# Attention and gated feed-forward in one kernel: K/Q and O/V weight loads issued at different places of the unit loop

## The chip, the cores and the metric

The kernel runs on one core of one Trainium2 chip. The metric is the device time of one execution in microseconds (us); lower is better. Engines are named as in the profile: PE (matmuls), PEld (its weight loads), DVE, ACT, POOL, and SP, which here computes nothing and issues every DMA.

## The reference, cut to what matters

Shapes: x is 16 x 256 x 256 (4096 tokens of width 256), 16 heads of 128, feed-forward width 2048 with 4-bit weights that are expanded first.

```python
def attn(x):
    q = einsum('bpd,hde->bphe', x, W_Q) + b_Q          # k and v likewise
    scores = einsum('bqhe,bkhe->bhqk', q, k) / sqrt(128)
    attn = softmax(where(causal, scores, -1e5), axis=-1)
    z = einsum('bkhe,bhqk->bqhe', v, attn)
    return einsum('bqhe,hed->bqd', z, W_O) + b_O

x = x + layernorm(attn(layernorm(x)))
x = x + layernorm(ffn(layernorm(x)))      # ffn: gelu(x Wg) * (x Wu), then Wd
```

## The kernel before, in words

Every fp32 matrix is kept as a rounded part and a remainder, and every product is three matmuls (`mm3`, line 353). The weights are split into the two parts once, in the first block of tokens (`w_split`, line 298), and written to DRAM (`w_keep`, line 324, some slots later, through the list `late`). In every later block they are read back, already split, by `w_get` (line 332): 512 KB for each of K, Q, O and for each half of a V tile. Each weight has two tiles in turn (`w_tile`, line 290).

The attention is cut into 128 **units**: 8 blocks of 512 tokens, 8 pairs of heads in each, 2 heads in a pair (`units`, `pairs`). The main loop runs `for i in range(-4, N + 2)` and works on several units at once; `p = i // 2` is the pair, and i is even for the first head of a pair. In the order of the program, one pass i does:

- `st_s(i+3)`: scores and the exponentials of unit i+3; then `st_qk(i+4)`: K and Q products of unit i+4 (weights K and Q of pair (i+4)//2).
- `st_t(i+3)`: DVE transposes the probabilities into `tr`.
- `st_o(p-1, i%2)`: output product of pair p-1 (weight O); `st_z(i)`: probabilities times V for unit i, which needs `ph` (ACT) and `pl` (POOL).
- `st_p(i+1)`: `ph` and `pl` of unit i+1, from `pt`; `st_v(i+4)`: V products, a quarter of those of two pairs (weight V).
- `st_b(i+2)`: SP issues the read `pt<-hop` (384 KB) of unit i+2; it must wait until the four writes of that unit have landed.
- `st_w(i+3)`: SP issues the four writes `hop<-tr` (96 KB each) of unit i+3.

So the probabilities of a unit go out to DRAM at the end of one pass and come back at the end of the next, and ACT, POOL and PE use them one and two passes after that. Between the stages stand calls of `slot`, in which side jobs advance by a step: layer norms of other blocks (which issue `xhop`, `xr`, `ohop`, `o`, `xs` and `x1d` transfers), the weight splits of the first block, the expansion of the feed-forward weights (`f_make`, `f_scale`, with the loads `ld` and the writes `fg`, `fu`, `fd`).

In the profile every computing instruction stands under line 99 (`run`) and every DMA issue under line 91 (`dma`), so the tile names tell them apart. `dma` ties each DMA to the one before it, so SP issues all of them in the order of the program. `w_get` of a later block also calls `overdue(now[0] + 4)`, which issues pending writes up to four slots early.

Where the weights are fetched (`weights`, defined after the first tokens are ready): at the end of odd passes, after `st_w`, O of pair p+1 and a V half for pair p+5; at the start of the next even pass, K and Q of pair p+3. Between the two stands only one `slot`, so the four loads are neighbours: 2 MB every second pass, none in the other. After the attention, the same core runs the feed-forward (the loop over `NGRP`).

Of the kernel before, what the change touches and what calls it, by code (L numbers as in the profile page):

```python
# [28 lines left out]
def kernel(  # L29
# [30 lines left out]
    def f(ap):  # L60
        return ap.bitcast(F32)
# [24 lines left out]
    def dma(dst, src):  # L86
        if queue[0] is None:
            queue[0] = nc.sync.dma_start(dst, src).ins
            return
        with tc.issue_after(queue[0]):  # L90
            queue[0] = nc.sync.dma_start(dst, src).ins  # L91
# [33 lines left out]
    def add(jobs, job, kind):  # L125
        jobs.append([job, 0, kind])

    def overdue(time):
        while late and late[0][0] <= time:
            _, do, args = late.popleft()  # L130
            do(*args)

    def slot(kinds, *lanes):

        now[0] += 1
        overdue(now[0])
        for jobs in lanes or (splits, urgent, behind, made, spare, idle):
            if step(jobs, kinds):
                return
# [91 lines left out]
    def ln1(b):  # L231
        xs = [x_load(x, b, hf) for hf in range(2)]
        yield V_, 7
        mv, rs = yield from ln_stats([xs[hf][:, t, :] for hf in range(2) for t in range(2)])
        xn = wide("xn")
        for t in range(4):
            yield G_
            ln_apply(xn[:, t, :], xs[t // 2][:, t % 2, :], mv, rs, t)
        yield V_
        hop = dram.tile([P, 4, 2 * P], F32, tag="xhop", name="xhop", bufs=2)  # L240
        yield from turn_tokens(hop, xn)
        yield N_, 5
        yield from split_tokens((1, b), hop)
# [46 lines left out]
    def w_tile(n):  # L290
        return wp.tile([P, 2, 1024 if n == "v" else 512], F32R, tag=f"w{n}", name=f"w{n}", bufs=2)

    def w_view(w):
        return w.rearrange("p s (k c) -> p s k c", k=2)
# [3 lines left out]
    def w_split(p, n):  # L298

        raw = RAW.pop((p, n)).rearrange("p (k c) -> p k c", k=2)  # L300
        key, done = p, True
        if n == "v":
            key, done = p // 2, p % 2
            w = HALF.pop(key) if done else w_tile(n)
            if not done:
                HALF[key] = w
            wv_ = w_view(w)[:, :, :, (p % 2) * 256 : (p % 2 + 1) * 256]
        else:
            w = w_tile(n)
            wv_ = w_view(w)  # L310
        c = qscale if n == "q" else 1.0
        run(nc.scalar.activation, wv_[:, 0], raw, AF.Copy, scale=c)
        if n in "vo":
            run(nc.gpsimd.tensor_tensor, wv_[:, 1], raw, f(wv_[:, 0]), ALU.subtract)
        else:
            run(nc.vector.scalar_tensor_tensor, wv_[:, 1], raw, c, f(wv_[:, 0]), ALU.mult, ALU.subtract)
        ahead = p + (2 if n == "v" else 1)
        if ahead < NG:
            w_raw(ahead, n)
        if done:  # L320
            W[key, n] = w_view(w)
            late.append((now[0] + 4, w_keep, (key, n, w)))
# [5 lines left out]
    def split(p, n):  # L328
        w_split(p, n)
        yield from ()  # L330

    def w_get(p, n):

        if p < NG:
            add(splits, split(p, n), A_ if n in "vo" else V_)
        elif p < len(pairs):
            overdue(now[0] + 4)
            if n == "v":
                key, part = p // 2, p % 2
                w = HALF.pop(key) if part else w_tile(n)  # L340
                HALF[key] = w
                dma(f(w[:, part]), WD[key % (NG // 2), n][:, part])
                if part:
                    W[key, n] = w_view(HALF.pop(key))
            else:
                w = w_tile(n)
                dma(f(w), WD[p % NG, n])
                W[p, n] = w_view(w)
# [110 lines left out]
    def st_t(u):  # L459


        pr = PR.pop(u)
        tr = work.tile([P, 4, 6, 32], F32, tag="tr", name="tr")
        run(
                nc.vector.transpose,
                tr.rearrange("p k m i -> p m k i"), pr.rearrange("p c b (k j) -> p (c b) k j", k=4)
            )
        TR[u] = tr
# [11 lines left out]
    def st_p(u):  # L480
        pt = PT.pop(u).rearrange("p a m i -> p m a i")
        ph = work.tile([P, 2, 2, P], F32R, tag="ph", name="ph")
        pl = work.tile([P, 2, 2, P], F32R, tag="pl", name="pl")
        four = [t.rearrange("p c b (a i) -> p (c b) a i", a=4) for t in (ph, pl)]
        run(nc.scalar.copy, four[0], pt[:, 0:4])
        run(nc.gpsimd.tensor_tensor, four[1], pt[:, 0:4], f(four[0]), ALU.subtract)
        PH[u] = (ph, pl, pt)
# [102 lines left out]
    def f_load(g, n):  # L590
        psrc, ssrc = FSRC[n]
        ld = work.tile([P, 2, 256], F32, tag="raw", name="ld", bufs=6)
        pk, sc = ld[:, 0, :].bitcast(I32), ld[:, 1, :]
        dma(pk, psrc[g])
        dma(sc, ssrc[g].unsqueeze(1).to_broadcast([8, 16, 256]))
        LD[g, n] = pk, sc

    def f_make(g, n, then):


        pk, sc = LD.pop((g, n))

        def small_tile(dtype, name):
            return work.tile([P, 2, 256], dtype, tag="code", name=name, bufs=4)

        c = work.tile([P, 2, 256], I32, tag="raw", name="codes", bufs=6)
        sg, t, v = small_tile(BF16, "sg"), small_tile(BF16, "t"), small_tile(BF16, "v")
        run(nc.vector.tensor_scalar, c[:, 0, :], pk, 15, None, ALU.bitwise_and)
        run(nc.vector.tensor_scalar, c[:, 1, :], pk, 4, 15, ALU.arith_shift_right, ALU.bitwise_and)
        yield V_  # L610
        if then:
            f_load(*then)
        run(nc.vector.tensor_scalar, sg, c, 8.0, -2.0, ALU.is_ge, ALU.mult)
        yield V_
        run(nc.vector.tensor_scalar, c, c, 7, None, ALU.bitwise_and)
        yield V_
        run(nc.vector.tensor_scalar, t, c, 2.0, 8.0, ALU.mult, ALU.subtract)
        yield V_
        run(nc.vector.scalar_tensor_tensor, v, c, 0.5, t, ALU.mult, ALU.max)
        yield V_  # L620
        run(nc.vector.scalar_tensor_tensor, v, c, 2.0, v, ALU.subtract, ALU.max)
        yield V_
        run(nc.vector.scalar_tensor_tensor, v, sg, 1.0, v, ALU.add, ALU.mult)
        add(made, f_scale(g, n, v, sc), G_)
# [316 lines left out]
    run(nc.gpsimd.tensor_scalar, bqs, bqk[:, 0, :], qscale, 1.0, ALU.mult, ALU.mult)  # L941
    for p in range(2):
        w_split(p, "v")
    w_get(2, "v")

    def weights(*of):
        for pn, n in of:
            if pn > {"o": -1, "v": 2}.get(n, 0):
                w_get(pn, n)

    for i in range(-4, N + 2):
        p = i // 2
        odd = i % 2 == 1
        if p >= 0 and not odd and p < len(pairs):
            b, g = pairs[p]
            if g == 0 and b + 1 < NBLK:
                add(urgent, ln1(b + 1), N_)
            if b == 0 and g == 7:
                pieces = [(fg, n) for fg in range(NG) for n in "gud"]
                f_load(*pieces[0])  # L960
                for m, piece in enumerate(pieces):
                    add(idle, f_make(*piece, pieces[m + 1] if m + 1 < len(pieces) else None), V_)
            if b == NBLK - 1 and g == 0:
                add(spare, x_ops(0), N_)
        if not odd:
            weights((p + 3, "k"), (p + 3, "q"))
        if 0 <= i + 3 < N:
            st_s(i + 3)
        slot(V_)
        if i + 4 < N:  # L970
            st_qk(i + 4)
        slot(V_, urgent, behind)
        slot(G_)
        slot(G_)
        if 0 <= i + 3 < N:
            st_t(i + 3)
        if 0 <= p - 1 < len(pairs):
            st_o(p - 1, i % 2)
        if 0 <= i < N:
            st_z(i)  # L980
        if 0 <= i + 1 < N:
            st_p(i + 1)
        if i + 4 < N:
            st_v(i + 4)
        elif after:
            run(*after.popleft())
        if 0 <= i + 2 < N:
            st_b(i + 2)
        if 0 <= i + 3 < N:
            st_w(i + 3)  # L990
        if odd:
            weights((p + 1, "o"), (p + 5, "v"))
        slot(A_ + G_)
        if N - 9 <= i < N - 7:
            f_get(0, "ug"[i - (N - 9)])
        if i >= N - 3:
            for name in (("m1",), ("m2",), ("m6",), (), ())[i - (N - 3)]:
                part(0, name)
# [93 lines left out]
```

## Time and profile before

| | |
|---|---|
| median of 3 runs | 1564.98 us (1562.86 to 1571.53) |
| profiled execution, its own time | 1558.9 us |
| its span, first to last instruction | 1556.9 us |
| mean granted PE clock | 0.994 |
| DMA moved | 407.54 MB, mean 262 GB/s |
| attention units, first K matmul of the first to that of the last | 10.9 to 1025.8 us |

How to read it: busy shares are averages over the whole span; in the views by stretch, a row gives the length, then each engine's busy time and number of instructions, the granted clock, the busy share of the 16 DMA engines and the rate. In a timeline a row gives start, duration, engine, operation, out<-in, and in brackets the idle time of the engine before it with what ended it. "SPq" is SP's queue of issues; its duration is that of the issue, not of the transfer.

### The profile page before, as it was taken

The numbers are of one execution on the slowest core, as the hardware profiler recorded it, in microseconds if no ns is written. First come the engines' busy times: TensorE is split into PE (matmuls) and PEld (weight loads), VectorE is DVE, ScalarE is ACT, GpSimd is POOL, SyncE is SP. The second block draws the span as 40 slices with busy tenths as digits, with TensorE's granted clock in tenths as the row PEclk, the third lists the DMA queues.
The fourth block names the chain that finished last, engine by engine and source line by source line (L and its number), as shares of the span: only waits on it lengthen the run. The fifth ranks groups of instructions, "written<-read, shape, count | busy, mean of one in ns | idle before, by whom it ended". The sixth has DMA issues, their size and how long they took to land.

```text
span 1556.9 us, 25639 instructions
## 1 busy us (share of the span) xinstructions
PE 1514.1 (97%) x7792; PEld 1278.6 (82%) x7792; DVE 1180.7 (76%) x2944; ACT 1028.6 (66%) x2600; POOL 807.1 (52%) x1017
## 2 busy tenths in 40 slices
PE   8999999999999999999999999999999999999996
PEld 6888888888888887888888888877788878878885
DVE  5775888877788786877877777867877777787765
ACT  5876666766767675766675666766566665665663
POOL 3754668667667765856875875981420230240100
PEclk9999999999999999999999999999999999999998
DMA  7998799998998988889889898986557555645551
GB/s 270 317 311 274 248 312 304 296 289 285 291 297 287 321 270 293 279 285 314 276 262 318 263 319 271 308 293 253 189 204 252 194 230 198 242 189 215 220 194 41
DMA packets 200409, 407.54 MB, mean 262 GB/s; under 512 B 21456, under 2 KB 128464, under 8 KB 189520
## 3 DMA queue, kind: packets, MB, share of 16 engines
q1 hardware_dynamic: 200272, 405.91, 76.7%
q8 instruction: 62, 1.02, 0.3%
q14 instruction: 75, 0.61, 0.1%
HBM read 294.15 MB, written 111.67 MB: 261 GB/s over the span
## 4 chain that ended last, share of the span: by engine, by line
PE 72%; DMA 11%; DVE 6%; ACT 5%; SPq 3%; issue 2%; POOL 1%; DVEq 0%; POOLq 0%; ACTq 0%
PE pd L99 11%; PE pk L99 9%; PE pv L99 8%; PE pq L99 8%; PE po L99 8%; PE sc L99 7%; PE pz L99 7%; PE pa L99 7%; PE pf L99 5%; DMA pt<-hop 4%; SPq L91 3%; DVE sum L99 3%; PE pe L99 2%; DMA hop<-tr 2%; DMA wq<-wq 1%
## 5 line engine op out<-in xcount | busy, mean ns | idle before, releaser
L99 POOL TENSOR_TENSOR pl<-pt,ph 128x512 fp32r<-128x512 f32 x128 | 165.0, 1289 | 246.2 <-ACT ph L99 234.9
L99 POOL TENSOR_SCALAR pr<-pr,rc 128x128 f32<-128x128 f32 (+1 forms) x512 | 248.6, 501 | 65.5 <-DVE rc L99 65.4
L99 ACT ACTIVATE pr<-sc,mn 128x128 f32<-128x128 f32 (+1 forms) x512 | 208.9, 422 | 74.4 <-DVE mn L99 68.2
L99 DVE CUSTOM_DVE_ANT_0 sc<-sc,mask 128x128 f32<-128x128 f32 (+1 forms) x512 | 180.5, 373 | 48.7 <-PE sc L99 39.6
L99 PE MATMUL pv<-wv,xT 128*128 128x512 f32 x768 | 210.2, 409 | 0.0
L99 PE MATMUL pd<-inter,wd 128*128 128x512 f32 x768 | 200.4, 394 | 5.3 <-ACT inter L99 4.0
L99 PE MATMUL pk<-xT,wk 128*128 128x512 f32 x768 | 200.4, 396 | 2.7 <-DMA wk<-wk 1.7
L99 PE MATMUL pq<-xT,wq 128*128 128x512 f32 x768 | 197.3, 392 | 0.1
L99 POOL TENSOR_TENSOR rs<-rs,mhalf 128x4 f32<-128x4 f32 (+1 forms) x33 | 35.1, 1063 | 288.9 <-DVE rs L99 288.9
L99 PEld LDWEIGHTS pd<-inter,wd 128*128 128x128 f32 x768 | 143.0, 189 | 42.8 <-DVE inter L99 7.0
L99 PEld LDWEIGHTS pq<-xT,wq 128*128 128x128 f32 x768 | 144.9, 189 | 33.5 <-PE pk L99 0.5
L99 ACT ACTIVATE zh<-pz,bqk 128x512 fp32r<-128x512 f32 x128 | 89.2, 697 | 116.3 <-PE pz L99 116.2
L99 PE MATMUL po<-zh,wo 128*128 128x512 f32 x512 | 157.7, 389 | 0.0
L99 PEld LDWEIGHTS pk<-xT,wk 128*128 128x128 f32 x768 | 135.8, 189 | 26.3 <-DMA wk<-wk 1.9
L99 PEld LDWEIGHTS pv<-wv,xT 128*128 128x128 f32 x768 | 135.8, 190 | 23.8
L99 ACT CAST ph<-pt 128x512 fp32r<-128x512 f32 x128 | 79.4, 620 | 113.0 <-DMA pt<-hop 112.1
L99 ACT COPY part<-pa 128x512 f32<-128x512 f32 x192 | 112.0, 586 | 62.4 <-PE pa L99 59.8
L99 ACT CAST inter<-sum 128x512 fp32r<-128x512 f32 x128 | 80.1, 626 | 101.1 <-DVE sum L99 101.0
L99 DVE TENSOR_TENSOR inter<-sum,inter 128x512 fp32r<-128x512 f32 x128 | 92.2, 720 | 58.9 <-ACT inter L99 55.9
L99 DVE SCALAR_TENSOR_TENSOR zl<-pz,bqk,zh 128x512 fp32r<-128x512 f32 x128 | 93.8, 733 | 51.7 <-ACT zh L99 51.4
L99 DVE STREAM_TRANSPOSE tr<-pr 128x768 f32<-128x768 f32 x128 | 123.4, 964 | 2.8 <-POOL pr L99 1.0
L99 DVE SCALAR_TENSOR_TENSOR kl<-pk,bqk,kh 128x512 fp32r<-128x512 f32 x128 | 95.8, 749 | 29.5 <-ACT kr L99 26.9
(139 smaller groups left out, 3815.8 us busy)
## 6 DMA issues: line engine op xcount, KB each, us to landing
hop<-tr SPq DMA_DIRECT2D x512, 96.0 KB
pt<-hop SPq DMA_DIRECT2D x128, 384.0 KB
wk<-wk SPq DMA_DIRECT2D x64, 512.0 KB
wq<-wq SPq DMA_DIRECT2D x64, 512.0 KB
wo<-wo SPq DMA_DIRECT2D x64, 512.0 KB
wu<-fu SPq DMA_DIRECT2D x32, 1024.0 KB
wg<-fg SPq DMA_DIRECT2D x32, 1024.0 KB
wv<-wv SPq DMA_DIRECT2D x56, 512.0 KB
```

Source lines behind the costliest of these rows:

```text
L91: queue[0] = nc.sync.dma_start(dst, src).ins
L99: ins = op(dst, *args, **kw)
```

## The change

The code before the loop adds K and Q of pair 1 to the fetches. In the loop, the fetch at the start of even passes goes. At the end of odd passes K and Q of pair p+4 are fetched instead of O and V; at the end of even passes O of pair p and the V half of pair p+4 are fetched. With i = 2p+1 the old code's next even pass has pair p+1 and fetched K and Q of (p+1)+3 = p+4, the same pair; O and V come one pass later than before.

```diff
-    w_get(2, "v")
+    for p, n in (2, "v"), (1, "k"), (1, "q"):
+        w_get(p, n)
...
-        if not odd:
-            weights((p + 3, "k"), (p + 3, "q"))
         if 0 <= i + 3 < N:
             st_s(i + 3)
...
         if 0 <= i + 3 < N:
             st_w(i + 3)
         if odd:
-            weights((p + 1, "o"), (p + 5, "v"))
+            weights((p + 4, "k"), (p + 4, "q"))
+        else:
+            weights((p, "o"), (p + 4, "v"))
         slot(A_ + G_)
```

## The prediction

> **What bounds the kernel now.** I read the page's shares first, then the waits, then the chain of work through one stall, then SP's issues around it.
>
> ```profile
> PE 1514.1 (97%) x7792; PEld 1278.6 (82%) x7792; DVE 1180.7 (76%) x2944; ACT 1028.6 (66%) x2600; POOL 807.1 (52%) x1017
> ```
>
> PE is the bound, so the change can win only what PE loses to waiting. The starts of the K matmuls (timeline of tile pk) give the length of each unit: an undisturbed one takes 7.83 us, and in the steady part, from unit 6 to the last, all but these are within 0.04 us of it. Lost time, us: unit 18: 2.02; 42: 2.01; 43: 1.89; 44: 0.91; 58: 0.80; 74: 2.02; 76: 2.25; 86: 1.64; 90: 2.79; 100: 0.30; 102: 1.94; 106: 4.31; 118: 2.49; 122: 0.36. From unit 42 on that is **23.7 us**, and but for 43 all of them are even units. What PE waits for, by the table of waits (engine, waited for, us in total, times, longest):
>
> ```profile
> PE pz L99 <- POOL pl L99: 9.2, 12, 0.9
> ...
> PE pk L99 <- DMA wk<-wk: 1.7, 1, 1.7
> ```
>
> The second row is unit 43. The first one is a chain; around unit 106 the chain of work (start, us, what) reads:
>
> ```profile
> 846.63 7.57 DMA wq<-wq
> ...
> 854.27 4.87 DMA pt<-hop
> ...
> 859.23 0.63 ACT ph L99
> ...
> 859.92 1.28 POOL pl L99
> ...
> 861.25 1.37 PE pz L99 x8
> ```
>
> PE waits for pl, that for ph, that for the read-back pt, and that had stood in SP's queue until a weight load landed. An ordinary pair of passes on SP's queue:
>
> ```profile
> 499.95 0.34 SPq L91 DMA_DIRECT2D pt<-hop  x1
> 500.38 2.09 SPq L91 DMA_DIRECT2D hop<-tr  x4
> 502.51 0.43 SPq L91 DMA_DIRECT2D wo<-wo  x1
> 502.99 0.45 SPq L91 DMA_DIRECT2D wv<-wv  x1
> 503.48 0.43 SPq L91 DMA_DIRECT2D wk<-wk  x1
> 503.95 0.57 SPq L91 DMA_DIRECT2D wq<-wq  x1
> 505.29 0.32 SPq L91 DMA_DIRECT2D pt<-hop  x1
> 505.88 2.13 SPq L91 DMA_DIRECT2D hop<-tr  x4
> ```
>
> The pt of 499.95 (odd unit 59) is used by ph at 504.83 without a wait, under 4.9 us later. The pt of 505.29 (even unit 60) has 2 MB just ahead of it: ph waits until 513.41, 8.1 us later. Its pl ends at 515.40 and PE reads it at 518.78, 3.4 us later; ph had waited 0.65, so an even unit's pt may keep ACT waiting about **4.1 us** before PE stalls (where ph did not wait at all, the gap from pl to PE is 4.14 us too). In the ten even units whose pt was later than that, ACT waited 4.5 to 6.6 us (idle before ph: units 38, 40, 54, 70, 72, 82, 86, 98, 102, 114: 5.2, 5.8, 4.5, 5.2, 5.5, 5.0, 6.5, 5.2, 6.6, 5.7); the unit of probabilities that is late is four behind the K matmuls that name a unit above, so 102 is the loss of 106. Odd units wait for pt by 1.0 us at most.
>
> **What the change does, part by part.**
>
> *O and V leave the burst ahead of the even pt.* The same loads remain, 1 MB per pass instead of 2 MB every second one. One MB takes, at the rate of stretches where the DMA share is full,
>
> ```profile
> 498.75:506.59 7.84, 7.84 (x47) 6.83 (x46) 7.66 (x19) 6.55 (x18) 5.54 (x7) 1.00 0.68 200
> 506.59:514.42 7.83, 7.83 (x46) 6.82 (x45) 5.99 (x22) 5.24 (x16) 6.03 (x9) 1.00 1.02 372
> ```
>
> (the last column is GB/s) 1.049 MB / 372 GB/s = **2.8 us**. The two rows show the alternation: 0.68 of the engines busy, then all. With 2.8 us off, the ten waits become 1.7 to 3.8 us, all below 4.1: no stall of this kind stays, 23.7 - 1.89 = 21.8 us. Unit 43's K was issued at 345.77 behind O, V and a 1 MB write; now O and V are not ahead of it, and it lands 2.8 us earlier against a wait of 1.7: its 1.89 goes too. Should only half the relief come, 1.4 us, waits of 5.8, 6.5 and 6.6 would still be 0.3, 1.0 and 1.1 us too long, some 3 us with the unit lengths growing more than PE's idle time (unit 106: 4.31 for 2.2 of idle); so the size matters little, the place does.
>
> The Trainium skill (DMA: Bandwidth & Descriptors, Anatomy of one DMA) fits a transfer as 2.0 us plus bytes at 436 GB/s; as an estimate from that page the relief is 2.4 us. No stretch here reaches that rate over a unit; the sum would lose under 0.5 us.
>
> *The odd pt gets 1 MB in front of it.* Its issue waits for the odd unit's four writes, which stand behind the burst today (last issued by 508.0, pt at 514.48). They lose 1 MB ahead; the pt gains 1 MB ahead. Both 2.8 us: it comes out even, and odd units have the whole 4.1 us free. Cost 0.
>
> *O and V come a pass later.* O would be issued after the even writes, about 508.1 in the rows above (505.88 plus 2.13), V 0.5 us after. PE first needs that O two passes on: 2.8 us into unit 64, which starts at 514.42, so 517.2, and V 2.4 us after that. That leaves **9.1 us** for O. From issue to landing, the chain of work shows loads behind today's burst at 5.1 (wo at 712.29), 6.4 to 7.6 (wv, wq) and 9.2 (one wk). Hidden in ordinary passes. The tiles were last read one pass earlier, so the issue itself waits for nothing new; today's O waits for an output product of its own pass, now gone. Behind O and V in SP's queue stand the layer norms' DMAs and the next pt, which waits for its writes anyway.
>
> *Where it is not hidden.* Once in a block SP issues ohop, xhop, o and xs (2 MB) between the odd pass's writes and the even pt; units 42, 58, 74, 90, 106 (11.9 of the 23.7 us). There pt comes 9 us later than usual, at 854.27 for unit 106. The queue also waits for weight loads that nothing in the next DMA reads:
>
> ```profile
> SPq L91 <- DMA wv<-wv: 33.4, 36, 2.9
> ...
> SPq L91 <- DMA wk<-wk: 32.8, 33, 2.1
> ```
>
> So SP goes no faster than its earlier transfers land, and with 1 MB fewer ahead pt goes out 2.8 us earlier, about 851.5. Its four writes take 1.9, so O goes out at 853.4, and PE wants it at 857.03 (first po row of that unit): 3.6 us. With 5.1 us to land it is 1.5 us late; in unit 90 the same 1.5; in 42, 58 and 74 the lead is 5.2 to 6 us and nothing is lost. Bounds: 0 (O lands in 3.6) and 4 us more each with 7.6 to land. I take 3 us minus what z would have waited there anyway: **+2 us**.
>
> *First block.* K and Q of a pair are now fetched just ahead of the first feed-forward load, where 0.5 MB of V was. DVE waits for that load today, and unit 18 is the result:
>
> ```profile
> DVE codes L99 <- DMA ld<-in_gp: 5.1, 1, 5.1
> ```
>
> 0.52 MB more at 372 GB/s: **+1.4 us** (0 to 2.8). The splits keep their kinds and slots, K and Q one pass sooner, O and V one later; the startup (units 0 to 5, 42 us) is bound by short DMAs and I know no row for it: 0, between -2 and +2. O's split then has 1.4 units until its use, which covers ACT's and POOL's 2 us. Writes of expanded weights that the K fetch pushes out early today are pushed at other places: 0, between -1 and +2. The feed-forward (from about 1053 us) issues nothing differently: 0.
>
> **Sum** against the profiled execution: -23.7 + 2 + 1.4 = -20.3; 1558.9 - 20.3 = 1538.6. The median stands 6.1 us above the profiled time; so **1545 us**.
>
> **Rivals.**
>
> *The block events stay.* SP's queue there may be paced by its 16 issues and by DVE's transposes instead of bytes; then pt goes out at 854.27 as now and O 1.9 us later, 0.9 us before PE wants it. The other units' 11.8 us are won, +1.4 lost, and O, 4 us late where z was 2.2 late, adds up to 8 over five events: -2, **1563 us**. For: SP issues one after the other, some 0.5 us each. Against: the chain names the landing of wq for 7.57 us of that stretch. 17%.
>
> *Bytes merely move.* The DMA engines are about 0.9 busy in the whole attention; if lateness comes from the total, stalls reappear in odd units: **1565 us**. Against: 200 GB/s in every second unit, 372 in the other. 5%.
>
> *Slower: O late in every pair.* The mechanism is the 9.1 us above. If O landed 10 us after its issue, PE would wait 0.9 us in each of some 55 pairs, 50 us against the 20 won: +30, **1595 us**; it decides from 9.6 us, where 55 x 0.5 eats the gain and the bound of a visible loss. For: one wk took 9.2. Against: that one stood behind a 1 MB write and O, V; O would stand behind 0.77 MB. The Trainium skill (same page, Rules for kernel authors) speaks for this rival: issue a DMA early and wait late. In no row does an O load come near its use today, so the trace neither bears it out nor excludes it. 6%.
>
> **How the numbers follow.** 72% for the forecast, alone 1539 (ld and O free, startup -2) to 1555 (half relief, O at its upper bound). The measurement of this kernel can tell about 0.5% (7.8 us) from no change. Faster: 0.72; same: 0.17 + 0.05 = 0.22; slower: 0.06. The range, 1539 to 1563, cuts the rival of the block events in half and leaves out the other two, about 0.19.
>
> **What would show it.** Right: units 42 to 122 at 7.83; ACT's idle time before even ph under 4 us; no "PE pz <- POOL pl" after unit 42; DMA shares of neighbouring units alike. Wrong: PE waiting for wo or wv; SP's pt in the block events not earlier; losses in odd units; unit 18 unchanged or worse than 5 us.

## The result and the profile after

The changed kernel takes 1546.2 us (median of 4 runs, 1540.65 to 1548.98) against 1564.5 us before: a ratio of 0.9859, 95% interval 0.9834 to 0.9884. Measured again beside the experiments, on two other occasions, it stood at 0.9831 (0.9794 to 0.9867) and 0.9862 (0.9839 to 0.9884). The profiled execution took 1548.52 us, span 1546.7; it is one of the longer of its runs, and the profile of the kernel before (1558.9 us) is shorter than any of its timed runs (the shortest: 1562.86). So the two profiles differ by 10.4 us where the medians differ by 18.3.

The page's first line, and the waits of PE (engine, waited for, us in total, times, longest us):

```profile
PE 1510.8 (98%) x7792; PEld 1281.4 (83%) x7792; DVE 1178.4 (76%) x2944; ACT 1033.0 (67%) x2600; POOL 810.1 (52%) x1017
```

```profile
PE po L99 <- DMA wo<-wo: 8.4, 6, 4.1
PE pd L99 <- ACT inter L99: 4.0, 4, 1.9
PE sc L99 <- DVE kl L99: 2.3, 1, 2.3
```

The wait for pl, 9.2 us before, is gone, and so is the one for wk. In their place stands one that the kernel before did not have: PE waits for the O weights. The chain of work around unit 106 (start, us, what) shows the exchange:

```profile
839.97 6.26 DMA wo<-wo
...
846.27 2.64 PE po L99 x6
848.91 1.74 PE pz L99 x10
```

Before, the chain went through wq, pt, ph and pl into pz; now pz follows po without a gap, and po has waited for its weights, which landed 6.3 us after their issue. SP's queue in an ordinary pair of passes:

```profile
500.35 0.32 SPq L91 DMA_DIRECT2D pt<-hop  x1
500.92 2.34 SPq L91 DMA_DIRECT2D hop<-tr  x4
503.30 0.45 SPq L91 DMA_DIRECT2D wo<-wo  x1
503.80 0.45 SPq L91 DMA_DIRECT2D wv<-wv  x1
...
508.14 0.33 SPq L91 DMA_DIRECT2D pt<-hop  x1
508.52 2.28 SPq L91 DMA_DIRECT2D hop<-tr  x4
511.59 0.34 SPq L91 DMA_DIRECT2D wk<-wk  x1
```

The two pt are 7.8 us apart, one unit; before they alternated, 5.3 and 9.2 us. The stretches of neighbouring units show the same in the last two columns (DMA share, GB/s; 0.68 and 200 against 1.02 and 372 before):

```profile
477.83:485.66 7.83, 7.83 (x46) 6.82 (x45) 7.29 (x19) 5.88 (x17) 7.72 (x10) 1.00 0.98 311
485.66:493.50 7.84, 7.84 (x46) 6.83 (x45) 6.12 (x18) 5.18 (x16) 7.84 (x9) 1.00 0.94 301
```

Where the time went, from the starts of the K matmuls (lost: over 7.833 us a unit) and the ends of the last po matmul, in the profiled executions:

| stretch | before, us | after, us | difference |
|---|---|---|---|
| span's start to unit 6 | 52.6 | 49.4 | -3.2 |
| lost in units 16 to 19 | 2.0 | 4.9 | +2.9 |
| lost in units 20 to 126 | 23.5 | 7.8 | -15.7 |
| start of unit 127 to the last po | 29.5 | 35.5 | +5.9 |
| last po to the end (feed-forward) | 501.5 | 501.3 | -0.2 |

The 7.8 us are units 26 (1.04), 44 (0.58), 74 (1.08), 76 (0.58) and 106 (4.06), each behind a wait for wo, unit 27 just behind 26 (0.17), and 58 (0.14) and 118 (0.23), which do not wait for wo.

### The profile page after: what moved, and what is told of

Same layout as the page of the kernel before. It is cut to its first block, busy times and chain, and to the rows that moved or that the text cites. A ratio compares the mean times of both kernels' runs of the same rounds, so it can differ in the third digit from the quotient of the medians.

```text
span 1546.7 us, 25648 instructions
## 1 busy us (share of the span) xinstructions
PE 1510.8 (98%) x7792; PEld 1281.4 (83%) x7792; DVE 1178.4 (76%) x2944; ACT 1033.0 (67%) x2600; POOL 810.1 (52%) x1017
## 3 DMA queue, kind: packets, MB, share of 16 engines
q8 instruction: 62, 1.02, 0.3%
## 4 chain that ended last, share of the span: by engine, by line
PE 80%; DMA 6%; DVE 5%; ACT 4%; SPq 2%; issue 1%; POOL 0%; DVEq 0%; POOLq 0%; ACTq 0%
PE pd L99 11%; PE po L99 10%; PE pk L99 10%; PE pv L99 10%; PE pq L99 9%; PE pz L99 9%; PE sc L99 8%; PE pa L99 7%; PE pf L99 5%; DVE sum L99 3%; DMA wo<-wo 2%; PE pe L99 2%; SPq L91 2%; ACT inter L99 1%; DMA hop<-tr 1%
## 5 line engine op out<-in xcount | busy, mean ns | idle before, releaser
L99 POOL TENSOR_SCALAR pr<-pr,rc 128x128 f32<-128x128 f32 (+1 forms) x512 | 251.7, 508 | 80.8 <-DVE rc L99 80.8
L99 PEld LDWEIGHTS po<-zh,wo 128*128 128x128 f32 x512 | 96.1, 189 | 31.1 <-DMA wo<-wo 11.5
L99 DVE SCALAR_TENSOR_TENSOR kl<-pk,bqk,kh 128x512 fp32r<-128x512 f32 x128 | 96.0, 750 | 30.3 <-ACT kr L99 27.1
```

The costliest lines, as they stand in the source:

```text
L99: ins = op(dst, *args, **kw)
```

## The experiments

The theory to test (A): PE lost its time to weight loads that stood ahead of the even units' pt, and what the changed kernel still loses is O arriving late because it is issued a pass later. Rival B: K and Q going ahead of O and V is what helped, not splitting the burst. Rival C: only the total DMA load counts.

**All four at the end of odd passes, in the new order.**

```diff
         if odd:
-            weights((p + 4, "k"), (p + 4, "q"))
-        else:
-            weights((p, "o"), (p + 4, "v"))
+            weights((p + 4, "k"), (p + 4, "q"), (p + 1, "o"), (p + 5, "v"))
```

> All four loads at the end of odd passes in the order K, Q, O, V: the burst of 2 MB is back, but in the changed kernel's order and with its places for K and Q. Theory A (bytes of weight loads ahead of an even unit's pt are what PE lost): even units stall again, ACT's idle time before even ph is over 4.1 us in about ten units, PE waits for pl and not for wo; 1555 to 1562 us, only startup and the K wait stay won. Rival B (the gain came from K and Q going ahead of O and V, not from splitting the burst): 1535 to 1546 us, no such waits. Rival C (the total DMA load decides, places do not matter): 1546 us.

Measured: 1584.05 us, 1.0103 (1.0077 to 1.0128) of the kernel before; PE waits for pl (9.9 us) and for ph (15.8 us), not for wo; ACT's idle time before even ph is over 4 us in twelve units from 34 on. B and C fall. A is right in kind, but it expected 1555 to 1562 us: units 20 to 126 lose 44.7 us, against 23.5 with the old burst of the same 2 MB. The five block events (units 42, 58, 74, 90, 106) grew from 11.9 to 29.8 us. The chain of work ahead of unit 90's loss:

```profile
739.78 6.84 DMA ohop<-oback
...
748.15 6.10 DMA pt<-hop
...
755.02 1.28 POOL pl L99
...
756.35 2.08 PE pz L99 x8
```

The kernel before had O and V ahead of ohop, K and Q behind. Here all four are ahead of it, its landing takes 6.8 us, the read `o<-ohop` is issued when it has landed, and pt stands behind the read. The wait itself is short in this unit, 0.2 us. Over the five block events, between the issue of the odd pt and that of the even one, SP waits 21.5 us for landings, against 13.0 in the kernel before: 16.7 against 12.9 for weight loads, 4.8 against 0.1 for ohop. The odd pt ahead also goes out 0.6 to 2.0 us later within its unit. So it is not only bytes ahead of pt that count, but also landings that SP waits for on the way. How the growth of 17.9 us divides between these is not shown, and no run moved ohop alone.

**O together with K and Q.**

```diff
         if odd:
-            weights((p + 4, "k"), (p + 4, "q"))
+            weights((p + 4, "k"), (p + 4, "q"), (p + 1, "o"))
         else:
-            weights((p, "o"), (p + 4, "v"))
+            weights((p + 4, "v"))
```

> K, Q and O (of pair p+1, a pass earlier than in the changed kernel) at the end of odd passes, V alone at the end of even ones: 1.5 MB and 0.5 MB. Theory A with its second half (what the changed kernel still loses is O coming a pass later): no PE wait for wo any more (8.4 us of idle time, some 13 us of lost time in the changed kernel's trace); even pt has 0.5 MB more ahead, 1.4 us, which only unit 102 (4.6 us of waiting already) cannot afford; about 1535 us. Rival B or C: 1546 us.

Measured: 1543.01 us, 0.9829 (0.9808 to 0.985); in the same measurements the kernel before took 1568.88. The expected 1535 us were missed, and the changed kernel's interval (0.9834 to 0.9884) overlaps, so the times do not part the two orders; the trace does. There is no wait for wo, and the end of the attention takes 31.2 us instead of 35.5. But units 42, 90 and 106 lose 1.4, 1.9 and 1.5 us to pt again, and unit 16 3.7 us, waiting for the tokens (xT) that ACT and POOL split. In the first block this order also moves the split of O; that this delays xT is likely, but no run shows it alone. The mechanism holds, the size does not: this order gives back about half of what it saves.

**V together with K and Q, O alone.**

```diff
         if odd:
-            weights((p + 4, "k"), (p + 4, "q"))
+            weights((p + 4, "k"), (p + 4, "q"), (p + 5, "v"))
         else:
-            weights((p, "o"), (p + 4, "v"))
+            weights((p, "o"))
```

> K, Q and V at the end of odd passes, O alone at the end of even ones. Theory A: O is as late as in the changed kernel, since only V stood behind it: PE waits 6 to 9 us in all for wo, and even pt waits 1.4 us longer; 1546 to 1550 us. If it is V's later place that costs, the time falls to about 1535 us. Rival C: 1546 us.

Measured: 1554.04 us, 0.9909 (0.9883 to 0.9936). V's place is not what costs: V comes a pass earlier, and the time does not fall. But theory A expected 1546 to 1550 us and a wait of 6 to 9 us for wo. O is later still, by the waits of PE:

```profile
PE po L99 <- DMA wo<-wo: 14.9, 8, 5.8
```

With the 0.5 MB of V ahead of pt, pt and O behind it go out 0.9 to 2.0 us later within the unit in four of the five block events (0.6 earlier in unit 74), and PE's wait for wo goes from 8.4 to 14.9 us.

**The changed kernel again**, beside the next three.

> The changed kernel once more, on the chip of the three below: about 0.986 of the kernel before. Theory A expects PE to wait for wo in the same places (units 26, 44, 74, 76, 106 and the end of the attention), more or less of it from run to run, and nowhere for pl after unit 42.

Measured: 1541.94 us, 0.9831 (0.9794 to 0.9867), kernel before 1569.04. The wait for wo is 8.0 us, in units 26, 28, 74, 76, 106 and at the end; the sum is close to that of the first profile, the units are partly others: this time 76 has the long one (3.98 us lost) and 106 a short one (0.59). Nothing waits for pl.

**The first feed-forward load ahead of K and Q.**

```diff
+        if i == 13:
+            f_load(*pieces[0])
         if odd:
             weights((p + 4, "k"), (p + 4, "q"))
...
-                f_load(*pieces[0])
```

The line taken out stood at the start of pass 14.

> The changed kernel with the first load of packed feed-forward weights issued at the end of pass 13 ahead of K and Q, not at the start of pass 14 behind them. Theory: the loss of units 18 and 19 (3.5 and 0.9 us in the changed kernel, 2.0 and 0 in the kernel before) is DVE waiting for that load, 1.4 us longer for 0.52 MB more ahead of it; here 1 MB goes from ahead of it to behind it, so units 18 and 19 lose under 1.5 us together, about 3 us less than the changed kernel. If the loss were DVE's own work it would stay at 4.4.

Measured: 1539.66 us, 0.9819 (0.9786 to 0.9851). Units 18 and 19 lose nothing. The loss was the load: DVE's wait for it, 5.1 us before and 5.9 us after the change, is 1.9 us here, and PE no longer feels it. The median is 2.3 us under the changed kernel's of the same series, and the intervals overlap.

**Old places in the first block, new ones from the second.**

```diff
+        if not odd and p + 3 < NG:
+            weights((p + 3, "k"), (p + 3, "q"))
...
         if odd:
-            weights((p + 4, "k"), (p + 4, "q"))
+            weights(*(w for w in ((p + 1, "o"), (p + 5, "v")) if w[0] < NG))
+            weights(*(w for w in ((p + 4, "k"), (p + 4, "q")) if w[0] >= NG))
         else:
-            weights((p, "o"), (p + 4, "v"))
+            weights(*(w for w in ((p, "o"), (p + 4, "v")) if w[0] >= NG))
```

Ahead of the loop this kernel again fetches V of pair 2 alone, without K and Q of pair 1.

> The old places for all fetches of the first block (the splits of pairs 0 to 7), the new ones from the second block on. Theory: the changed kernel's startup gain (units 0, 4 and 5 together 3.2 us shorter) came from K and Q being split a pass earlier; here units 4 and 5 go back to 8.2 and 7.4 us and the time is 2 to 3 us above the changed kernel's. Units 42 to 126 as in the changed kernel.

Measured: 1546.77 us, 0.9859 (0.983 to 0.9889), 4.8 us over the changed kernel's median of the same series, with intervals that overlap. The profile is clearer: units 4 and 5 take 9.0 and 7.4 us, against 6.7 and 6.4 to 6.5 in every profile with the new order; unit 6 starts at 52.8 us, as before the change (52.6).

**O at the start of even passes**, half a pass earlier, behind ohop and ahead of xhop, o, xs and pt.

```diff
+        if not odd and p >= NG:
+            weights((p, "o"))
         if 0 <= i + 3 < N:
             st_s(i + 3)
...
         else:
-            weights((p, "o"), (p + 4, "v"))
+            if p < NG:
+                weights((p, "o"))
+            weights((p + 4, "v"))
```

> From the second block on, O is issued at the start of the even pass, half a pass earlier than in the changed kernel: behind ohop, but ahead of xhop, o, xs and pt; the first block as in the changed kernel. Theory A: O has landed before PE needs it in units 74, 106 and at the end of the attention, PE waits for wo under 1 us in all; the even pt has 0.5 MB more ahead (1.4 us), which costs under 1.5 us each in the block events and nothing elsewhere; 1535 to 1538 us. If O's lateness came from the total traffic, PE still waits 5 us or more for wo.

Measured: 1536.86 us, 0.9804 (0.977 to 0.9838). No wait for wo; what PE waits for now, longest first:

```profile
PE pd L99 <- ACT inter L99: 3.9, 4, 1.9
PE sc L99 <- ACT qr L99: 2.3, 4, 1.0
PE pz L99 <- POOL pl L99: 2.3, 5, 0.8
```

Units 20 to 126 lose 3.3 us (90, 102 and 106, for pt), the end of the attention takes 29.9 us, near the 29.5 before the change. O's lateness was its place in the queue. By the times alone this kernel does not yet stand apart from the changed one of its series (0.9794 to 0.9867).

**Both repairs**, and the changed kernel beside it.

> O at the start of the even pass (second block on) and the first feed-forward load ahead of K and Q: the two repairs together. Theory A: units 18 and 19 lose under 1 us, no wait for wo, 1 to 2 us each left in units 90, 102, 106; 2 to 3 us under the kernel with O at the even start alone, so about 1534 us and 0.978 of the kernel before. If the two repairs only shift the same DMA time about, the time stays at 1537.

> The changed kernel on the same chip as the run with both repairs: 0.983 to 0.986 of the kernel before, 6 to 9 us above the kernel with both repairs.

Measured: 1536.3 us (0.9806, 0.9781 to 0.983) against 1546.84 us (0.9862, 0.9839 to 0.9884) for the changed kernel: faster than both kernels, by intervals that do not meet. Units 18 and 19 lose nothing; DVE's wait for the load, 5.9 us in the changed kernel, reads here:

```profile
DVE codes L99 <- DMA ld<-in_gp: 1.5, 1, 1.5
```

The second repair does not show beside the first in the medians (1536.9 and 1536.3, in different series; about 1534 was expected). Units 16 to 19 lose 1.7 us less than with the first repair alone, but units 20 to 126 lose 5.2 us instead of 3.3 (units 44, 86 and 118 are new among them). So the other expectation, that the two repairs only shift the same DMA time about, is not excluded. A third tile for O, which would leave 1 MB in each pass and still fetch O early, needs about 1 KB a partition more than there is, so it has no time.

## Why the prediction was right

Forecast 1545 us, measured 1546.2. The main mechanism was right; that the number agrees so closely is luck in part. The sum was made against the profiled execution, and there the change gained 10.4 us, half of the forecast 20.3: O's lateness cost 13.4 us instead of 2 and the first feed-forward load 2.9 instead of 1.4, while the startup gave 3.2 that was not forecast. The medians moved further, by 18.3 us (27.1 and 20.6 in the two later measurements), because the profile before stands 5.6 us under its median and the profile after 2.3 us above its own. What those 8 us are in the timed runs, no trace shows. One of the prediction's own signs of being wrong did come: PE waits for wo.

*The even pt, -21.8, and the K wait, -1.9*: right. No unit from 20 on waits for pl or wk; ACT's longest idle time before an even ph is 4.6 us (unit 102, where PE was itself waiting for O), before 6.6. The other nine of the ten long waits fell to 2.9 us at most (forecast: 1.7 to 3.8). Splitting the burst is the cause, not the order: with the burst back, in the new order, the waits come back. The Trainium skill's fit that the prediction sets beside this (DMA: Bandwidth & Descriptors, Anatomy of one DMA) was measured for DMAs that GpSimd issues. Here SP issues all of them, and the 512 KB loads of the prediction took 5.1 to 9.2 us from issue to landing in a full queue, where that fit gives 3.2 us as an estimate.

*The odd pt, 0*: right, though it did not come out even: ACT's idle time before an odd ph is now up to 3.4 us, before 1.0, still under the 4.1 that are free. Of the odd units from 7 on only 19 and 27 lose anything (0.9 and 0.2 us), just behind the stalls of 18 and 26, and no odd pt makes PE wait.

*O a pass later, hidden in ordinary passes; +2 in the block events*: the term that was mis-sized. It is 7.5 us in the loop and 5.9 at the end of the attention. The lead of O in unit 106 was worked out right (3.6 us; measured 3.9, from 839.97 to 843.90, which is the unit's start and the 2.77 us that the kernel before took to its first po). Its landing was not: 5.1 us taken, 6.3 measured, and PE's idle 2.2 us cost 4.1, with the granted clock at 0.86 (below). Unit 90, forecast to lose as much as 106, lost nothing; its O had 5.2 us. Unit 74, forecast with at least 5.2 us, had 4.2 and lost 1.1, and the units 26, 44 and 76 outside the block events lost time too. And the end of the attention got no term: "issues nothing differently" holds for the feed-forward but not for the passes before it. There the units have fewer stages and are shorter, so a pass of lead is fewer us: O went out at 1027.78 behind xhop, pt and four writes, and po waited 4.1 us. With O fetched half a pass earlier both losses went.

```profile
1027.78 4.36 DMA wo<-wo
...
1032.19 2.93 PE po L99 x6
```

*First feed-forward load, +1.4 (0 to 2.8)*: right in kind; units 16 to 19 lost 2.9 us more than before in this profile, 0.4 and 2.5 more in the other two of the changed kernel. DVE's own wait grew by 0.8 us only (5.0 and 5.5 us in the other two, 5.1 before).

*Startup, 0 (-2 to +2)*: wrong, -3.2. K and Q split a pass earlier shorten units 4 and 5, by 2.4 us here, as the run with the old first block shows. It was not short DMAs alone that bound them: before, PE waited there for pl and for ACT's qr (0.8, 0.4 and 0.6 us), after, for neither. The remaining 0.8 us are unit 0, which takes 5.4 to 8.2 us from profile to profile with the same startup, so they are not shown to be the change's.

*The rivals.* That the block events stay: no, pt of unit 102 goes out 3.6 us ahead of the start of unit 106, where before it went out with it; in all five events it is 2.7 to 5.7 us earlier within the unit. The step behind that was only partly the one forecast. Between the odd and the even pt SP's waits for landings fell just from 13.0 to 11.0 us over the five events, and two issues of some 0.5 us are gone. Most of the gain, 1.9 to 3.7 us, is that the odd pt ahead goes out earlier already. It waits for the four writes of its unit, and this wait of SP (before, then after) is the one that fell most:

```profile
SPq L91 <- DMA hop<-tr: 223.8, 146, 7.8
...
SPq L91 <- DMA hop<-tr: 136.4, 150, 4.1
```

That bytes merely move: no, and the run with the burst restored excludes it. That O is late in every pair: no, in 5 of some 55, but in the run with V among K and Q, where O goes out later, it is late in 7. The Trainium skill's rule that the prediction weighed there (DMA: Bandwidth & Descriptors, Rules for kernel authors: issue early, wait late) is borne out for O, with 8.4 us of waits and some 13 us lost, but it is not the whole story here: the burst with O and V issued earlier cost 23.5 us, because other transfers stood behind it.

## What to carry to other kernels

In a queue that issues in order, ask of each bulk prefetch not only how early it is but what stands behind it: spread bulk loads over the passes, behind the small transfers that the next stage waits for, and look at what lands ahead of each transfer that the queue itself waits for. When a load is moved later, compare its lead with its landing time under the busiest neighbours, and check the last passes apart, where the passes are shorter. A wait that is short for the pipeline can cost twice its length if the clock falls.

## What the runs showed of the hardware

After PE waits of some 2 us the granted clock is sometimes lower over the unit. The third column from the end is the clock; unit 106 waited 2.2 us and lost 4.1, unit 74 waited 0.8 and lost 1.1:

```profile
841.13:853.02 11.89, 9.68 (x46) 8.03 (x45) 7.54 (x21) 7.07 (x19) 7.04 (x11) 0.86 0.99 333
588.83:597.74 8.91, 8.13 (x47) 6.75 (x46) 7.08 (x19) 5.61 (x16) 4.30 (x6) 1.00 1.03 362
```

In the third profile of the changed kernel a wait of 1.8 us came with a lower clock (0.85, 3.7 us lost), while with V among K and Q a wait of 2.1 us did not:

```profile
849.06:859.29 10.23, 8.12 (x46) 6.74 (x45) 6.94 (x19) 7.06 (x19) 6.71 (x11) 1.00 1.00 336
```

In the kernel before, two waits of 1.35 and 0.85 us in unit 106 came with a clock of 0.86 and 4.3 us lost, two of 1.24 and 0.84 us in unit 90 with 1.00 and 2.8 us. So the length alone does not decide, and what else does is not shown. The Trainium skill (TensorE: Matmul & The Clock Gate, Why this matters for your kernels) asks for no idle gaps over about 3 us; here 1.8 us of idle between the records was enough.
